# Two cross-attention layers: queries split by batch, a power on GpSimd, and layer two's residual on ScalarE and GpSimd

## The chip, the core and the metric

The kernel runs on one core of one Trainium2 chip. The metric is device time in microseconds, the median of several runs. Five engines work side by side, each in the order of its own instructions: TensorE (PE in the profile; its weight loads are PEld), VectorE (DVE), ScalarE (ACT), GpSimd (POOL) and SyncE (SP), which here only issues DMAs.

## What is computed

64 sequences x of 256 tokens and 320 channels pass through two cross-attention layers, each with a context of 77 tokens and 512 channels (the last 4 are image tokens), 20 heads of 16 channels. All is float32. Cut to what matters:

```python
# layer one (index 0 in the code): all 77 context tokens are text, its image part is empty
q, k, v = heads(x @ Wq.T), heads(text @ Wk.T), heads(text @ Wv.T)
out = softmax(q @ k.T * scale) @ v    # per head, merged
x = out @ Wo.T + bo + x
# layer two (index 1): 73 text tokens, and attention over 4 image tokens steered by it
probs_t = softmax(q @ k_t.T * scale)
text_out = probs_t @ v_t
qsem = l2norm(probs_t @ text)        # the mean context that each query saw
sem = qsem @ l2norm(ip).T
probs_ip = softmax(q @ k_ip.T * scale + 0.5 * sem) * spatial_mask
x = (text_out + probs_ip @ v_ip) @ W_out + b_out + x
```

In this data the context of both layers is the same tensor. The l2norm of `qsem` needs one over a square root for each query and head; the kernel gets the squared norm from a Gram matrix of the context.

## The kernel before

**Staging.** The 64 sequences are 32 pairs p. A pair's work is cut into units of 128 queries and eight heads; `UNITS` lists five for each of its two batches b, so ten units make a pair in each layer. The main loop (L1061) runs over steps g; p, k = divmod(g, 10), so a *period* is ten steps, k = 0 to 9, and "step 3" means k = 3. In step g layer one works on unit g and layer two on unit g - 13.

**A step, in the order in which it is written.** First `drains` (L1071): the copies and sums that take finished projections out of PSUM. Then the products of the Gram matrix for layer two (`semantics`, L769 and L776) and the scores of both layers (`scores`, L650) into one PSUM tile `sc`, which has one buffer of four banks; VectorE takes off the maxima (`shifted`, L668 and L670). Then layer two's exponentials of the step before are turned by TensorE (`transposed(1)`, L718 and L719) and copied by ScalarE (L725, L726); then ScalarE's exponential of layer one (L678), VectorE's products with the Gram part (L787, L790), the first group of `fillers`, layer one's transposes (`transposed(0)`, L718 and L719, copied at L744 and L745 or, for the fifth unit, L733 and L736), ScalarE's copy of the sums (L1057) and layer two's exponentials (L681, L682), the normalisation of layer one on VectorE and GpSimd (L695, L696, L702, L705), VectorE's sum over the products (L1130), the second group of fillers, `attend` (L807, L810, copied at L830 and L833) and the third group. In steps 9 and 4 layer two's batch 0 or 1 has its last unit, and `image_squares` (L868, L869), `text_output` (L842, three L860) and, at the step's very end, `image_norm` (L873, L875) are added; the step after has `image_scores` (L881 to L883).

**Fillers** (L950) are the projections, spread by hand over the ten steps and over three places in a step. `queries` (L584) and `project` (L597) begin with `halves` (L530): it makes eight matmuls of 128x256 (L538) for both batches at once and returns `rest` (L543), the last channels (L548), which runs in the drains of the next step. Then ScalarE copies the queries to SBUF (L593), or VectorE adds bias and residual to the output (`out_of`, L608). `project_last` (L616) makes the last 64 output channels (L623, L627). `queries` of layer two stands in step 3, that of layer one in step 4, both in the second group; `project` of layer two in step 9, with its drain in step 0; `project_last` of layer two in step 0, first group, beside the Gram matrix (`gram`, L506, copied at L509).

**What sets the order.** `keep_order` (L54) ties the instructions of PE, ACT, DVE and POOL to the order in which they are written, and those of SP up to step 13. Later DMAs of SP may be placed by the scheduler; they are issued in the order of that queue.

**PSUM.** `sc` holds four banks. Pool `ptr` has two buffers of one bank with the tag `tr`, and each `transposed` takes both: one for four transposes, one for the fifth. Pool `pms` has two buffers with the tag `ms`, for all projections and `attend` (which takes one `tr` for batch 1).

**The square root.** `image_norm` takes ScalarE's square root and behind it calls one exponential of a single element. In the trace each of the two begins with an ACT_TABLE_LOAD, at L873 and L875; the exponentials at L678 have none after it.

Of the kernel before, what the change touches and what calls it, by code (L numbers as in the profile page):

```python
# [14 lines left out]
H = 20  # L15
# [56 lines left out]
def tile_two_cross_attentions(ctx: ExitStack, tc: tile.TileContext, a: dict, out: bass.AP):  # L72
# [265 lines left out]
    def image_norms():  # L338
        sq = wkip.rearrange("p k c -> p (k c)")[:, : KE * NIP * NB].rearrange("p (k t) -> p k t", k=KE)
        nc.vector.tensor_mul(sq, cip, cip)  # L340
        ps = pms.tile([P, 512], F32, tag="ms", name="ss_ps")
        for k in range(KE):
            nc.tensor.matmul(ps[:, : NIP * NB], ones, sq[:, k, :], start=(k == 0), stop=(k == KE - 1))
        nc.vector.tensor_scalar_max(rip, ps[:, : NIP * NB], EPS * EPS)
        nc.scalar.activation(rip, rip, AF.Sqrt)
        nc.vector.reciprocal(rip, rip)


# [181 lines left out]
    def halves(name, w, src):  # L530


        main, last = src
        ps = [pms.tile([P, 2, S], F32, tag="ms", name=f"{name}_{b}") for b in range(2)]
        for b in range(2):
            for k in range(2):
                for m in range(2):
                    nc.tensor.matmul(  # L538
                        ps[b][:, m, :], w[:, k, m * P : (m + 1) * P], main[:, k, b * S : (b + 1) * S],
                        start=(k == 0 and m == 0), stop=False,  # L540
                    )

        def rest():  # L543
            for m in range(2):
                for b in range(2):
                    rows = slice(b * HALF, (b + 1) * HALF)
                    for c in halves_of(P):
                        nc.tensor.matmul(  # L548
                            ps[b][c, m, :], w[rows, 2 + b, m * P + c.start : m * P + c.stop], last[rows, :],
                            start=False, stop=(m == 1),  # L550
                        )
            return ps

        return rest

    held = {}

# [25 lines left out]

    def queries(l, p):  # L584

        rest = halves(f"q_ps{l}_{p}", wq[l], xts[p])

        def end():
            ps = rest()
            q = big.tile([P, 2, S2], F32, tag=f"q{l}", name=f"q{l}_{p}", bufs=2 - l)  # L590
            for m in range(2):
                qs[l, p, m] = q[:, m, :]
            return [lambda b=b: nc.scalar.copy(q[:, :, b * S : (b + 1) * S], ps[b]) for b in range(2)]  # L593

        held["q"] = end

    def project(l, p):  # L597

        rest = halves(f"o_ps{l}_{p}", wo[l], aTs[l, p])

        def end():
            ps = rest()

            def out_of(m):
                to = xts[p][0][:, m, :]
                for b in range(2):
                    t = to[:, b * S : (b + 1) * S]
                    nc.vector.scalar_tensor_tensor(t, ps[b][:, m, :], bo[l][:, m : m + 1], t, ALU.add, ALU.add)  # L608
                if l:
                    nc.sync.dma_start(out[m * P : (m + 1) * P, p * S2 : (p + 1) * S2], to)  # L610

            return [lambda m=m: out_of(m) for m in range(2)]

        held["o"] = end

# [177 lines left out]
    def attend(p, b):  # L793


        if (0, p) not in aTs:
            aTs[0, p] = channels("aT0", f"aT0_{p}", 1)
        main, last = aTs[0, p]
        banks = [
            pool.tile([P, 2, S], F32, tag=tag, name=f"pv{p}_{b}_{i}")  # L800
            for i, (pool, tag) in enumerate(((pms, "ms"), (ptr, "tr") if b else (pms, "ms")))
        ]

        rows = [slice(j * PAD, (j + 1) * PAD) for j in range(4)]

        def head_pairs(to, b, r, part, pt, start):
            nc.tensor.matmul(to, v0s[b][0][:, r, part].rearrange("p e d -> p (e d)"), pt, start=start, stop=False)  # L807

        def rests(to, b, r, part, rt, stop):
            nc.tensor.matmul(  # L810
                to, v0s[b][1][rows[r], part].rearrange("p e d -> p (e d)"), rt[rows[r]], start=False, stop=stop
            )

        for i in range(2):
            for j in range(4):
                r = (j + 2 * i) % 4
                head_pairs(banks[i][rows[j], 0, :], b, r, i, pts[0, i][0][:, r, :], True)
            for j in range(4 if b else 0):
                pt = pts[0, 2, j // 2][0][:, j % 2, i * P : (i + 1) * P]
                head_pairs(banks[i][rows[j], 1, :P], j // 2, j % 2, 2, pt, False)  # L820
        for j in range(4):
            for i in range(2):
                r = (j + 2 * i) % 4
                rests(banks[i][rows[j], 0, :], b, r, i, pts[0, i][1], not b)
        if b:
            for j in range(4):
                for s in range(2):
                    rests(banks[s][rows[j], 1, :P], j // 2, (j + 2 * s) % 4, 2, pts[0, 2, j // 2][1], True)
        for i in range(2):
            nc.scalar.copy(main[:, i, b * S : (b + 1) * S], banks[i][:, 0, :])  # L830
        if b:
            for s in range(2):
                nc.scalar.copy(last[:, s * P : (s + 1) * P], banks[s][:, 1, :P])  # L833
# [11 lines left out]
            lasts[p] = big.tile([P, 2, 2, H - HT, D], F32, tag="an_last", name=f"an_last{p}", bufs=1)  # L845
        by_head((an[:, 0], lasts[p][:, :, b], an[:, 1]), sums[:, :, NIP : NIP + D], rec)

    one = const.tile([P, 1], F32, tag="one", name="one")

    def by_head(to, t, factor):  # L850

# [18 lines left out]

    def image_norm(p, b):
        r = stats[p, b][2]
        nc.scalar.activation(r, r, AF.Sqrt, scale=(SCALE / SEM) ** 2)  # L873

        nc.scalar.activation(one, r[:, :1], AF.Exp, scale=0.0)  # L875

    def image_scores(p, b):

        att, sums, r = stats[p, b]
        num = nums[p, b] = small.tile(full, F32, tag="num", name=f"num{p}_{b}", bufs=2)  # L880
        nc.vector.reciprocal(r, r)  # L881
        nc.gpsimd.tensor_mul(num, sums[:, :, :NIP], r.unsqueeze(2).broadcast_to(full))
        nc.gpsimd.tensor_add(num, num, att)  # L883

# [65 lines left out]
    def fillers(k, p):  # L950
# [8 lines left out]
        if k == 0:  # L959
# [2 lines left out]
                    add(0, p, value_rows, 0, l)  # L962
                add(1, p, values, 0, p, 0)
            add(0, p - 1, gram, p - 1, 0)
            add(0, p - 3, project_last, 1, p - 3)
            if p:
                add(2, p, place_values, 0, p, 0)
            add(2, p - 1, values, 1, p - 1, 0)
# [21 lines left out]
        elif k == 3:  # L990
            add(0, p + 1, load_context, p + 1)
            if p == 0:
                add(1, p, image_keys, 0)
            add(1, p - 1, queries, 1, p - 1)
            add(1, p, place_values, 0, p, 1)
            add(1, p - 1, keys_by_head, 1, p - 1, 1)
        elif k == 4:
            if p == 0:
                add(0, p, image_keys, 1)
            add(1, p - 1, values, 1, p - 1, 1)  # L1000
            add(1, p + 1, queries, 0, p + 1)
        elif k == 5:
            if p == 0:
                add(0, p, image_keys, 2)
            add(0, p + 1, keys, 0, p + 1, 0)
            add(0, p - 1, gram, p - 1, 1)
        elif k == 6:
            while len(made_rows) * P < min(NB, 2 * (p + 2)) * T:
                rows_todo.extend((len(made_rows), l) for l in range(2))
                made_rows.append(rows_todo[-1])  # L1010
            for n in range(len(rows_todo) // 2):
                add(0, p, value_rows, *rows_todo.pop(0))
            if p == 0:
                add(0, p, image_norms)
            else:
                add(1, p, keys, 1, p, 0)
            add(0, p - 1, gram_out, 1)
            for b in range(2):
                add(1, p - 2, place_image_values, b)
        elif k == 7:  # L1020
            add(0, p + 1, keys, 0, p + 1, 1)
            add(1, p + 1, last_keys, p + 1)
            if p:
                add(2, p, keys, 1, p, 1)
            add(2, p, place_image_keys, p)
            add(1, p - 2, lambda: made.update(wT=image_transposed(p - 2)))
            if p == 0:
                add(1, p, image_rows)
        elif k == 8:
            while rows_todo:  # L1030
                add(0, p, value_rows, *rows_todo.pop(0))
            add(1, p - 1, place_gram, 1)
            add(1, p + 1, keys_by_head, 0, p + 1, 0)
            add(1, p - 1, place_values, 1, p - 1, 1)
            add(2, p - 2, lambda: held.update(i=outputs(p - 2)))
        else:
            add(0, p - 2, project, 1, p - 2)
            add(1, p + 1, values, 0, p + 1, 0)
            for b in range(2):
                add(1, p - 1, image_values, p - 1, b)  # L1040
# [9 lines left out]
    last_keys(0)  # L1050
    keys_by_head(0, 0, 0)
    queries(0, 0)
    for fn in held.pop("q")():
        fn()

# [148 lines left out]
```

## Time and profile before

| | us |
|---|---|
| median of 3 runs (2475.21 to 2477.18) | 2475.45 |
| the profiled execution | 2475.09 |
| its span in the trace | 2473.3 |
| PE busy | 2354.1 |
| DVE busy | 2001.3 |
| ACT busy | 1493.8 |
| POOL busy | 1178.5 |
| table loads of L873 and L875, 64 each of 1283 ns | 164.2 |
| L608, 256 of 461 ns | 102.7 |

The rows are read so: busy time is the sum of an engine's instructions, and an engine can be busy and still not set the end. The chain of waits follows the work that ended last back through what released it. The timeline lists instructions by start (us from the span's start), duration, engine, line, tiles written and read, and in brackets how long the engine had been idle and what ended that. The granted TensorE clock of this execution was 0.999 of full speed.

### The profile page before, as it was taken

The numbers are of one execution on the slowest core, as the hardware profiler recorded it, in microseconds if no ns is written. First come the engines' busy times: TensorE is split into PE (matmuls) and PEld (weight loads), VectorE is DVE, ScalarE is ACT, GpSimd is POOL, SyncE is SP. The second block draws the span as 40 slices with busy tenths as digits, with TensorE's granted clock in tenths as the row PEclk, the third lists the DMA queues.
The fourth block names the chain that finished last, engine by engine and source line by source line (L and its number), as shares of the span: only waits on it lengthen the run. The fifth ranks groups of instructions, "written<-read, shape, count | busy, mean of one in ns | idle before, by whom it ended". The sixth has DMA issues, their size and how long they took to land.

```text
span 2473.3 us, 97920 instructions
## 1 busy us (share of the span) xinstructions
PE 2354.1 (95%) x41374; PEld 1839.1 (74%) x41374; DVE 2001.3 (81%) x3677; ACT 1493.8 (60%) x3813; POOL 1178.5 (48%) x2621
## 2 busy tenths in 40 slices
PE   7989999999999999999999999999999999999888
PEld 5677777777777777777777777777777777777666
DVE  4588888888888888888888888888888888888864
ACT  3466666666666666666666666666666666666543
POOL 2345445545445445445545445545454545445432
PEclk9999999999999999999999999999999999999999
DMA  6202211111211111211111211111211111211000
GB/s 176 73 22 58 64 42 46 47 49 53 65 41 47 46 50 52 67 41 46 46 49 52 67 42 46 46 49 52 66 43 46 46 48 51 65 39 34 21 21 25
DMA packets 163451, 126.22 MB, mean 51 GB/s; under 512 B 72517, under 2 KB 146629, under 8 KB 163013
## 3 DMA queue, kind: packets, MB, share of 16 engines
q1 hardware_dynamic: 162148, 118.81, 16.8%
q8 instruction: 326, 5.34, 0.9%
q10 hardware_dynamic: 864, 1.15, 0.2%
q14 instruction: 113, 0.92, 0.1%
HBM read 79.56 MB, written 37.89 MB: 47 GB/s over the span
## 4 chain that ended last, share of the span: by engine, by line
PE 69%; DVE 21%; ACT 7%; issue 2%; POOL 1%; DMA 0%; SPq 0%; DVEq 0%; ACTq 0%; POOLq 0%
PE tr L718 9%; PE sc L769 8%; DVE w L670 6%; PE sc L650 6%; PE o_ps L538 5%; PE q_ps L538 5%; PE k_ps L359 4%; PE v_ps L401 4%; PE o_ps L623 4%; PE pv L807 3%; DVE mx L668 3%; PE sc L776 3%; ACT w L678 3%; PE q_ps L566 2%; DVE prod L787 2%; DVE sm L695 2%
## 5 line engine op out<-in xcount | busy, mean ns | idle before, releaser
L668 DVE TENSOR_REDUCE mx<-sc 128x8 f32<-128x584 f32 (+1 forms) x640 | 496.7, 776 | 308.7 <-PE sc L650 305.6
L670 DVE TENSOR_TENSOR w<-sc,mx 128x616 f32<-128x616 f32 x640 | 511.8, 800 | 73.4 <-ACT kT L362 0.5
L718 PE MATMUL tr<-ident,parts 128*128 128x128 f32 x2560 | 407.5, 282 | 55.7 <-ACT pt L725 49.0
L718 PEld LDWEIGHTS tr<-ident,parts 128*128 128x128 f32 x2560 | 280.2, 141 | 176.1 <-issue 76.1
L725 ACT COPY pt<-tr 128x512 f32<-128x512 f32 x320 | 187.4, 586 | 321.4 <-PE tr L718 321.4
L702 POOL TENSOR_TENSOR parts<-w,sm 128x104 f32<-128x104 f32 (+1 forms) x352 | 122.5, 352 | 536.1 <-ACT parts L682 152.6
L705 POOL TENSOR_TENSOR parts<-w,sm 128x512 f32<-128x512 f32 x320 | 337.0, 1053 | 0.0
L678 ACT ACTIVATE w<-w 128x616 f32<-128x616 f32 x320 | 229.8, 718 | 144.2 <-DVE w L670 144.2
L769 PEld LDWEIGHTS sc<-gv,pt 64*64 64x64 f32 x10240 | 232.9, 133 | 85.8 <-ACT sums L1057 31.5
L769 PE MATMUL sc<-gv,pt 64*64 64x94 f32 x10240 | 277.2, 245 | 13.2 <-ACT sums L1057 12.5
L695 DVE TENSOR_REDUCE sm<-w 128x8 f32<-128x616 f32 x320 | 251.2, 785 | 34.5 <-ACT w L678 34.5
L650 PE MATMUL sc<-kbd,q 32*64 32x154 f32 x10240 | 247.3, 293 | 1.1 <-ACT q L593 1.0
L685 POOL COPY att<-w 128x32 f32<-128x32 f32 x320 | 67.4, 210 | 377.0 <-DVE w L670 377.0
L538 PE MATMUL o_ps<-aT,wo 128*128 128x256 f32 x1024 | 231.8, 379 | 0.7 <-ACT aT L943 0.7
L538 PE MATMUL q_ps<-x,wq 128*128 128x256 f32 x1024 | 231.6, 379 | 0.0
L1130 DVE TENSOR_REDUCE nrm<-prod 128x8 f32<-128x584 f32 x320 | 226.7, 709 | 0.3
L787 DVE TENSOR_TENSOR prod<-sc,parts 128x512 f32<-128x512 f32 x320 | 217.8, 681 | 2.8 <-PE sc L776 2.8
L1057 ACT COPY sums<-sc 128x168 f32<-128x168 f32 x320 | 97.3, 304 | 200.3 <-DVE prod L790 198.5
L538 PEld LDWEIGHTS o_ps<-aT,wo 128*128 128x128 f32 x1024 | 189.6, 190 | 24.5 <-ACT aT L943 1.2
L681 ACT ACTIVATE parts<-w 128x512 f32<-128x512 f32 x320 | 207.3, 648 | 0.3 <-DVE w L670 0.2
L538 PEld LDWEIGHTS q_ps<-x,wq 128*128 128x128 f32 x1024 | 189.6, 190 | 23.1
L744 ACT COPY pt<-tr 128x512 f32<-128x512 f32 x256 | 149.6, 584 | 68.7 <-PE tr L718 68.6
(139 smaller groups left out, 4471.4 us busy)
## 6 DMA issues: line engine op xcount, KB each, us to landing
out_dram<-x SPq DMA_DIRECT2D x64, 256.0 KB
x<-in_x_dram SPq DMA_DIRECT2D x31, 512.0 KB
v_rows<-vs SPq DMA_DIRECT2D x76, 192.0 KB
vm<-v_rows SPq DMA_DIRECT2D x64, 192.0 KB
ct<-in_ctx_dram SPq DMA_DIRECT2D x32, 308.0 KB
cf<-in_ctx_dram SPq DMA_DIRECT2D x38, 256.0 KB
vq<-v_rows SPq DMA_DIRECT2D x128, 48.0 KB
v_rest<-v_rows SPq DMA_DIRECT2D x256, 9.8 KB
```

Of the source, the lines that this page charges most:

```text
L538: nc.tensor.matmul(ps[b][:, m, :], w[:, k, m * P : (m + 1) * P], main[:, k, b * S : (b + 1) * S], start=(k == 0 and m == 0), stop=False,)
L650: nc.tensor.matmul(ps[c, r, 2 * T * l : 2 * T * (l + 1)], tokens[rows, c], kbd[rows, part].rearrange("p e t -> p (e t)"), start=start, sto ...
L668: nc.vector.tensor_reduce(mx, sc[:, :, :, :nt], AX.X, ALU.max)
L670: nc.vector.tensor_tensor(w, sc, mx.unsqueeze(3).broadcast_to([P, 4, 2, T]), ALU.subtract)
L678: nc.scalar.activation(w, w, AF.Exp, scale=SCALE)
L681: nc.scalar.activation(two[:, :4].rearrange("p (e a) j t -> p (a j) e t", e=2), w[:, :, :, :M], AF.Exp, scale=SCALE)
L695: nc.vector.tensor_reduce(sm, w, AX.X, ALU.add)
L705: nc.gpsimd.tensor_tensor(two[:, : 4 * P].rearrange("p (h t) -> p h t", h=8), w[:, :, :, :M].rearrange("p j g t -> p (j g) t"), sm.rearran ...
L718: nc.tensor.transpose(ps[:, i, :], flat[:, i * P : (i + 1) * P], ident)
L769: nc.tensor.matmul(ps[c, i % 2 * 2 + j, at : at + GV], pt[half_rows, i, c], gv[b][half_rows, part, i, :], start=start and i < 2, stop=False,)
L787: nc.vector.tensor_tensor(prod[:, :, :, :M], sm[:, :, :, :M], w[:, :4].rearrange("p (e a) j t -> p (a j) e t", e=2), ALU.mult)
L1130: nc.vector.tensor_reduce(eight(stats[q, b][2], u), prod, AX.X, ALU.add)
```

## The change

1. `halves` no longer makes both batches' matmuls. It returns `batch(b)`, which takes a bank and makes the four matmuls of one batch, and `rest`. `queries` makes batch 0 where it is called; a new filler `second_batch` makes batch 1. In steps 3 and 4 `queries` moves to the first group, ahead of layer one's transposes, and `second_batch` takes its old place behind them. `project` makes both batches at once, as it did.
2. `image_norm` raises the squared norms to the power -0.5 on GpSimd (one instruction on 128x40 elements, with a constant tile `power`, issued at the end of the step, so in step 9 just ahead of step 0's drains). ScalarE's square root and its dummy exponential, and VectorE's reciprocal in `image_scores`, are gone. The constant factor moves to the one square root made at the start (L345).
3. Layer two's output is taken out of PSUM by ScalarE with the bias (two activations of 128x256 for each batch, into a tile `o` of one buffer), and GpSimd adds it to x in SBUF (128x512 for each batch). The output DMAs follow behind both. Layer one's stays on VectorE, now batch by batch.
4. `project_last` of layer two moves from the first to the second group of step 0, behind layer one's transposes. In `attend` the products of the fifth unit come behind the main products of both banks instead of between them.

```diff
@@ image_norms
-        nc.scalar.activation(rip, rip, AF.Sqrt)
+        nc.scalar.activation(rip, rip, AF.Sqrt, scale=(SCALE / SEM) ** 2)
@@ halves
-        ps = [pms.tile([P, 2, S], F32, tag="ms", name=f"{name}_{b}") for b in range(2)]
-        for b in range(2):
+        ps = []
+
+        def batch(b):
+            ps.append(pms.tile([P, 2, S], F32, tag="ms", name=f"{name}_{b}"))
             for k in range(2):
...
-        return rest
+        return batch, rest
@@ queries
-        rest = halves(f"q_ps{l}_{p}", wq[l], xts[p])
+        batch, rest = halves(f"q_ps{l}_{p}", wq[l], xts[p])
+        batch(0)
+        held["batch"] = lambda: (batch(1), held.update(q=end))
...
-        held["q"] = end
+    def second_batch():
+        held.pop("batch")()
@@ project
-            def out_of(m):
-                to = xts[p][0][:, m, :]
-                for b in range(2):
-                    t = to[:, b * S : (b + 1) * S]
+            to = xts[p][0]
+
+            def out_of(b):
+                for m in range(2):
+                    t = to[:, m, b * S : (b + 1) * S]
                     nc.vector.scalar_tensor_tensor(t, ps[b][:, m, :], bo[l][:, m : m + 1], t, ALU.add, ALU.add)
-                if l:
-                    nc.sync.dma_start(out[m * P : (m + 1) * P, p * S2 : (p + 1) * S2], to)
-
-            return [lambda m=m: out_of(m) for m in range(2)]
+
+            def with_bias(b):
+                o = big.tile([P, 2, S], F32, tag="o", name=f"o{p}_{b}", bufs=1)
+                for m in range(2):
+                    nc.scalar.activation(o[:, m], ps[b][:, m, :], AF.Identity, bias=bo[l][:, m : m + 1])
+                t = to[:, :, b * S : (b + 1) * S]
+                nc.gpsimd.tensor_tensor(t, t, o, ALU.add)
+
+            def store():
+                for m in range(2):
+                    nc.sync.dma_start(out[m * P : (m + 1) * P, p * S2 : (p + 1) * S2], to[:, m])
+
+            return [lambda b=b: (out_of, with_bias)[l](b) for b in range(2)] + [store] * l
@@ attend
-            for j in range(4 if b else 0):
+        for i in range(2 * b):
+            for j in range(4):
@@ image_norm, image_scores
-        nc.scalar.activation(r, r, AF.Sqrt, scale=(SCALE / SEM) ** 2)
-        nc.scalar.activation(one, r[:, :1], AF.Exp, scale=0.0)
+        nc.gpsimd.tensor_tensor(r, r, power, ALU.pow)
...
-        nc.vector.reciprocal(r, r)
@@ fillers
-            add(0, p - 3, project_last, 1, p - 3)
+            add(1, p - 3, project_last, 1, p - 3)
...
-            add(1, p - 1, queries, 1, p - 1)
+            add(0, p - 1, queries, 1, p - 1)
+            add(1, p - 1, second_batch)
...
-            add(1, p + 1, queries, 0, p + 1)
+            add(0, p + 1, queries, 0, p + 1)
+            add(1, p + 1, second_batch)
```

## The prediction

> **What bounds the kernel now.** I read the page's busy shares and chain first, then what TensorE waits for, then the timeline of one period around 1200 to 1282 us. A period is the ten steps of one pair of batches. The shares:
>
> ```profile
> PE 2354.1 (95%) x41374; PEld 1839.1 (74%) x41374; DVE 2001.3 (81%) x3677; ACT 1493.8 (60%) x3813; POOL 1178.5 (48%) x2621
> ...
> PE 69%; DVE 21%; ACT 7%; issue 2%; POOL 1%; DMA 0%; SPq 0%; DVEq 0%; ACTq 0%; POOLq 0%
> ```
>
> TensorE is busy 95% of the span, so all its idle time is about 119 us. What ends TensorE's waits (columns: total us, times, longest):
>
> ```profile
> PE tr L718 <- ACT pt L725: 49.0, 66, 1.9
> PE sc L769 <- ACT sums L1057: 12.5, 28, 1.6
> PE k_ps L359 <- ACT q L593: 12.5, 29, 0.4
> PE g_ps L506 <- DVE x L608: 7.0, 29, 0.6
> ```
>
> The reader is to see that the first row is the prize and that 29 is the number of full periods. In the timeline (start, us, engine, line) the first row is this, in step 3:
>
> ```profile
> 1201.99 0.59 ACT L725 COPY pt<-tr 128x512 f32<-128x512 f32 x1 [1.92 <-PE tr L718]
> ...
> 1202.72 0.63 PE L718 MATMUL tr<-ident,parts 128*128 128x128 f32 x4 [0.71 <-ACT pt L725]
> ```
>
> Layer two's transposes fill both `tr` banks, and layer one's must wait until ScalarE has emptied the first. Steps 3 and 4 each lose 0.71 us so. A period is 73.1 us (score matmuls L650 at 1208.68 and 1281.80).
>
> **Queries split by batch (steps 3 and 4).** The same 16 matmul records of L538 (3.62 us together) are issued, but half of them, about 1.7 us, now stand between the two groups of transposes. The copies end at 1202.74, and TensorE, at work until about 1203.6, no longer waits. I count 62 such places (31 and 32 query projections, the last in the drain): 62 x 0.71 = 44 us. The first bank must be free 1.7 us earlier: in step 3 its last reader ended at 1200.06 (L580), in step 4 the query copies of L593 end before the transposes do. Cover holds at both.
>
> **Power in place of square root.** ScalarE loses, twice a period, two table loads of 1.28 us (L873, L875) and two small activations (236 and 203 ns); VectorE loses a reciprocal of 353 ns. In step 9 and in most of step 4 this lies beside TensorE's work. What surfaces is in step 5: the query copies stood behind the loads until 1218.07, and the keys (L359) began at 1218.69. Moving both query halves up by 1.42 us and dropping the loads, I get keys at 1216.75 (where layer two's transposes of step 5 then end), layer one's transposes at 1218.3 (after L359 and L506), then ScalarE's two copies (0.59, 0.27), the exponential (0.72) and the sums (0.30): the next semantic matmuls (L769) start at about 1220.9 instead of 1222.63. That is 1.73, of which 1.42 is counted; 0.31 x 29 = 9 us. What is late next there is the sums copy L1057, as today. **Gains: 53 us.**
>
> The power itself stands on no row. Call it X. From below: L901, a GpSimd product of the same 128x40, 0.25 us. From above: the whole route it replaces, 1.28 + 0.24 + 1.28 + 0.20 + 0.35 = 3.35 us. I take 1.0, four passes of the nearest row, since a power is not one product. In step 5 GpSimd is idle for about 2.5 us behind it (L860 ends at 1218.36, its next work starts at 1220.88), so there X costs nothing. In step 0 it does.
>
> **Layer two's residual, and the order of step 0.** VectorE loses four L608 (1.55 us at 1251.67). ScalarE gains four activations of 128x256 and GpSimd two sums of 128x512. The tile `o` has one buffer. So the second batch's first activation waits for the first batch's sum on GpSimd, and the changed program carries that wait. GpSimd's order before that sum is text output (three L860), the power, the sum. Behind the waiting activation stand, on ScalarE, L725 and L726, which empty the banks that layer one's transposes need, then the exponential, the Gram copy and all else of step 0. Rows of the period today:
>
> ```profile
> 1251.36 0.39 DVE L842 RECIPROCAL rec<-sums 128x40 f32<-128x40 f32 x1
> ...
> 1251.89 0.63 POOL L860 TENSOR_TENSOR an<-sums,rec 128x256 f32<-128x256 f32 x1 [0.51 <-DVE rec L842]
> ...
> 1252.85 0.64 POOL L860 TENSOR_TENSOR an<-sums,rec 128x256 f32<-128x256 f32 x1
> ...
> 1253.85 0.57 ACT L725 COPY pt<-tr 128x512 f32<-128x512 f32 x1
> ...
> 1255.08 0.66 PE L718 MATMUL tr<-ident,parts 128*128 128x128 f32 x4
> ...
> 1258.22 0.88 PE L769 MATMUL sc<-gv,pt 64*64 64x94 f32 x32
> ```
>
> The reader is to see that GpSimd is occupied until 1253.49, because it waits for a reciprocal at the end of VectorE's chain; none of the edits moves that chain, which starts at step 9's scores. From there:
> - power: 1253.49 + X;
> - first sum, by L705 (128x512, 1.05 us): 1254.55 + X;
> - the second batch's two activations, by L830 (two 128x256 in 0.65 to 0.7 us): 1255.25 + X;
> - L725 (0.59): layer one's transposes start at 1255.85 + X instead of 1255.08;
> - today 3.14 us pass from there to the next L769. The last output part (L623, 1.45 us) used to stand before these transposes and now stands after them: 4.59 us. L769 at 1260.44 + X against 1258.22.
>
> Step 0 thus loses 2.2 + X, although L506 no longer waits for L608. The part 2 products moved behind in `attend` cost nothing: their copies (L733, L736) end before the main products do. The output DMAs move behind the second sum, to about 1256.6 + X; on SP's queue the Gram stores, the next values and x stand behind them, and the first consumer (x, loaded in step 2 for step 4) has over 10 us. The sums' 2.1 us on GpSimd hide before its next due work, the normalisation, which itself waits for the exponential.
>
> **The clock.** TensorE would idle from the end of L506 (about 1253.3) to 1255.85 + X, at X = 1 for 3.5 us. The trace has one stretch like this, in the drain: nothing from 2452.85 to 2455.62, 2.77 us. One-microsecond windows (PE busy first, then the other engines; PEclk is the granted clock):
>
> ```profile
> 2454.00:2455.00 1.00, 0.00 (x0) 0.00 (x0) 0.00 (x0) 0.00 (x0) 0.84 (x3) 1.00 0.00 0
> ...
> 2458.00:2459.00 1.00, 1.00 (x8) 0.67 (x7) 0.00 (x0) 0.00 (x0) 0.00 (x0) 0.50 0.00 0
> ```
>
> From about 2457.0 to 2460.5 the clock was halved, 3.5 us that give 1.75 us of work less. One sample does not say how often a stretch of 3 to 4 us does this, so none and every period are the bounds (0 and 29 x 1.75 = 51 us) and I take half, 25 us.
>
> The Trainium skill, "TensorE: Matmul & The Clock Gate", Part 1, says that the clock halves after an idle window of about 3.4 us, and that windows run freely. By that page 3.5 us of idleness would hardly ever hold a whole window, the term would be near 0, and the forecast 25 us lower; by the trace's one row, where 2.77 us sufficed, it would be 25 us higher.
>
> **The sum.** 29 x (2.2 + 1.0) = 93; clock 25; gains 53; in the tail the chain activation, sum, activation, sum (0.7 + 1.05 + 0.7 + 1.05 = 3.5) replaces four L608 (1.66): 2. Net 93 + 25 - 53 + 2 = 67. The profiled execution took 2475.09 (span 2473.3), the median of the runs is 2475.45, so they agree. **2475 + 67 = 2542 us.** Its own range: X = 0.25 and no clock term, 71 - 53 + 2 = 20, so 2495; X = 3.35 and every period halved, 161 + 51 - 53 + 2 = 161, so 2636.
>
> **Rivals.**
> - *Step 0's wait is cheaper than the splits bring (faster).* It decides at 51 / 29 = 1.76 us a period. For it: L869, just before the reciprocal, took 0.94 us at 1250.50 beside GpSimd's L705, but 0.20 elsewhere; free of that, text output starts 0.74 earlier, and with X = 0.25 step 0 loses 1.71. If the sums' wait (12.5 us, second row) also goes, the time is 2475 + 50 - 53 + 2 - 12 = 2462; with no hold-up at all 2475 - 53 - 12 = 2410. Against it: nothing here moves L705 away from L869. Chance 0.14.
> - *The two cancel*: the same without the last 12, 2475 +- 5. Chance 0.07.
> - *The power is long (slower still)*: a software routine above 3.35 us. Each us costs 29 us in step 0, and beyond 2.5 us also holds up step 5: 2640 to 2900. For it: no row bounds it truly. Against: GpSimd's rows of this shape are all 0.2 to 0.3 us. Chance 0.07.
> - *The forecast*, 2495 to 2636: 0.72.
>
> **Numbers.** The range 2470 to 2636 takes in the forecast's bounds and the cancelling case, 0.79 or so. Faster by over 0.2% (about what a measurement of this kernel can tell from no change) 0.14, within it 0.07, slower 0.79.
>
> **What would show it.** Right: no `tr` wait on L725 in steps 3 and 4; in step 0 the second batch's activation waiting for GpSimd for about 2 to 4 us, and layer one's transposes of step 0 behind L725 with a new TensorE gap of 2.5 us + X; table loads down to the first few; power's own duration read off directly; PEclk below 1 after the gap, or not. Wrong: step 0 not longer than today, which would mean that the first sum runs before 1254 or that the transposes don't stand behind it.

## The result and the profile after

| | us |
|---|---|
| before, 4 runs (2472.68 to 2477.18) | 2475.33 |
| after, 4 runs (2802.06 to 2804.03) | 2803.45 |
| ratio, 95% interval | 1.1326 [1.1306, 1.1345] |
| after, span in the trace | 2800.3 |
| after, granted TensorE clock | 0.938 of full speed |

The change costs 328 us. The direction was forecast; the size lies far above the range. The busy shares and the chain of the page after:

```profile
PE 2396.6 (86%) x41374; PEld 1865.2 (67%) x41374; DVE 1948.9 (70%) x3485; ACT 1362.1 (49%) x3685; POOL 1686.7 (60%) x2750
...
PE 54%; POOL 20%; DVE 16%; issue 5%; ACT 4%; DMA 0%; SPq 0%; POOLq 0%; DVEq 0%; ACTq 0%
```

TensorE now stands idle for 404 us (2800.3 - 2396.6) instead of 119, and GpSimd, which had 1% of the chain, has 20% of it. Line numbers have moved: `tr` is now L734 and L735 (copies L741, L742, L749), the semantic products L785, layer one's normalisation on GpSimd L718 and L721, text output L878, the sums copy L1075; new are the power (L891), the activations into `o` (L620) and the sums on GpSimd (L622). What TensorE waits for (total us, times, longest):

```profile
PE tr L734 <- ACT pt L741: 293.6, 36, 10.0
PE tr L734 <- POOL parts L721: 35.2, 27, 2.1
PE sc L785 <- ACT sums L1075: 24.8, 31, 3.6
```

Thirty of the 36 waits in the first row are one and the same place, 9.65 us in each period. The rows of the keys (12.5 us before) and of the Gram matmuls (7.0) are gone. So is the wait of steps 3 and 4, as the timeline of a step 3 shows (start, us, engine, line):

```profile
1424.67 0.59 ACT L741 COPY pt<-tr 128x512 f32<-128x512 f32 x1 [1.92 <-PE tr L734]
...
1426.25 0.60 PE L734 MATMUL tr<-ident,parts 128*128 128x128 f32 x4
```

The transposes have no bracket: TensorE came to them from the first half of the queries, which ends after the copy. The groups (busy us and mean ns, then the idle time before them) name what ScalarE waited for:

```profile
L891 POOL TENSOR_TENSOR nrm<-nrm,power 128x40 f32<-128x40 f32 x64 | 434.6, 6790 | 0.0
...
L620 ACT ACTIVATE o<-o_ps,bo 128x256 f32<-128x256 f32 x128 | 53.9, 478 | 312.0 <-POOL x L622 304.8
```

The power takes 6.79 us, 27 times the product of the same 128x40 (0.25 us). In the timeline of one step 0 the whole chain can be read downwards:

```profile
1475.02 0.63 POOL L878 TENSOR_TENSOR an<-sums,rec 128x256 f32<-128x256 f32 x1
1475.61 6.79 POOL L891 TENSOR_TENSOR nrm<-nrm,power 128x40 f32<-128x40 f32 x1
1482.37 1.25 POOL L622 TENSOR_TENSOR x<-x,o 128x512 f32<-128x512 f32 x1
1483.66 0.84 ACT L620 ACTIVATE o<-o_ps,bo 128x256 f32<-128x256 f32 x2 [9.88 <-POOL x L622]
1484.39 0.58 ACT L741 COPY pt<-tr 128x512 f32<-128x512 f32 x1
...
1485.12 1.09 PE L734 MATMUL tr<-ident,parts 128*128 128x128 f32 x4 [9.65 <-ACT pt L741]
...
1490.87 0.88 PE L785 MATMUL sc<-gv,pt 64*64 64x94 f32 x32
```

Text output ends at 1475.65; the power runs to 1482.40; only then comes the first sum, then the second batch's activations, which waited 9.88 us for the one buffer of `o`; then L741, and behind it TensorE. The clock follows (window, its length, busy time of PE, PEld, DVE, ACT, POOL, then granted clock, DMA share and GB/s):

```profile
1475.00:1477.00 2.00, 0.47 (x8) 0.32 (x5) 1.76 (x4) 0.00 (x0) 2.00 (x3) 1.00 0.00 0
1479.00:1481.00 2.00, 0.00 (x0) 0.00 (x0) 0.00 (x0) 0.00 (x0) 2.00 (x1) 0.50 0.00 0
1487.00:1488.00 1.00, 1.00 (x8) 0.54 (x6) 0.44 (x1) 0.89 (x3) 1.00 (x2) 0.50 0.44 158
1489.00:1490.00 1.00, 1.00 (x32) 0.61 (x20) 0.23 (x1) 0.00 (x0) 0.43 (x1) 1.00 0.07 14
```

TensorE's last matmul ends at 1475.48. The clock is halved from about 1478 until after 1488, so TensorE also works slowly for some 3 us once it is let go: the four transposes at 1485.12 take 1.09 us instead of the 0.66 of the prediction's row, and they do so in all 30 periods. The Trainium skill, "TensorE: Matmul & The Clock Gate", Part 1, says that the clock halves after an idle window of about 3.4 us of a free-running counter; a stretch of 9.65 us fits that in any position. But the clock was down 2.4 us after the last matmul here, and 2.1 to 4.7 us after it over the 29 full periods: idleness shorter than the page's window was enough, and the measurement decides.

Step 0 is not equally long in all periods: 18.4 us in some, 19.4 in others, 20.2 at most. The clock accounts for that. Here are two periods, in which the transposes begin at 310.87 and at 394.01, each seen some three us later:

```profile
314.00:315.00 1.00, 1.00 (x18) 0.44 (x18) 0.47 (x1) 0.00 (x0) 0.92 (x3) 1.00 0.07 11
397.00:398.00 1.00, 1.00 (x6) 0.24 (x2) 0.00 (x0) 0.00 (x0) 0.92 (x3) 0.50 0.08 16
```

In the first the clock came back 3.0 us after the transposes began, in the second 5.2; step 0 took 18.40 and 19.43 us. In all 29 full periods step 0, less half of its time at the halved clock behind the gap, is 16.8 to 17.2 us.

In step 5 the power does not hold up TensorE, but step 6 pays:

```profile
1440.10 6.80 POOL L891 TENSOR_TENSOR nrm<-nrm,power 128x40 f32<-128x40 f32 x1
...
1447.72 1.04 POOL L721 TENSOR_TENSOR parts<-w,sm 128x512 f32<-128x512 f32 x1
...
1448.82 0.66 PE L734 MATMUL tr<-ident,parts 128*128 128x128 f32 x4 [1.27 <-POOL parts L721]
...
1451.29 0.88 PE L785 MATMUL sc<-gv,pt 64*64 64x94 f32 x32 [0.70 <-ACT sums L1075]
```

Layer one's normalisation (L721) stands behind the power on GpSimd, and TensorE waits twice for what follows from it. The lengths of the steps, from a step's first score matmul to the next step's (medians over the middle of the trace, step 0 after the change the mean of 29 periods, us), put the loss in its places:

| kernel | 3 | 4 | 5 | 6 | 0 | 1 | time |
|---|---|---|---|---|---|---|---|
| before | 8.13 | 8.13 | 6.80 | 6.47 | 7.89 | 7.22 | 2475 |
| after | 7.23 | 7.23 | 6.25 | 8.33 | 18.94 | 7.23 | 2803 |

Steps 2, 7, 8 and 9 are the same in both. A period gains 2.35 us in steps 3 to 5 and loses 1.86 in step 6 and about 11.1 in step 0. In six of the 29 full periods step 6 took 8.21 us before the change already and loses next to nothing; over all 29 it loses 42 us.

### The profile page after: what moved, and what is told of

It reads as the page before. It is cut to its first block, busy times and chain, and to the rows that moved or that the text cites. A ratio compares the mean times of both kernels' runs of the same rounds, so it can differ in the third digit from the quotient of the medians.

```text
span 2800.3 us, 97864 instructions
## 1 busy us (share of the span) xinstructions
PE 2396.6 (86%) x41374; PEld 1865.2 (67%) x41374; DVE 1948.9 (70%) x3485; ACT 1362.1 (49%) x3685; POOL 1686.7 (60%) x2750
## 4 chain that ended last, share of the span: by engine, by line
PE 54%; POOL 20%; DVE 16%; issue 5%; ACT 4%; DMA 0%; SPq 0%; POOLq 0%; DVEq 0%; ACTq 0%
POOL nrm L891 12%; PE tr L734 7%; PE sc L785 6%; PE sc L666 5%; PE o_ps L639 4%; PE q_ps L540 4%; PE o_ps L540 4%; DVE w L686 4%; PE v_ps L401 3%; POOL an L878 3%; PE k_ps L359 2%; PE sc L792 2%; DVE prod L803 2%; DVE mx L684 2%; PE q_ps L568 2%
## 5 line engine op out<-in xcount | busy, mean ns | idle before, releaser
L734 PE MATMUL tr<-ident,parts 128*128 128x128 f32 x2560 | 420.4, 288 | 329.5 <-ACT pt L741 293.6
L734 PEld LDWEIGHTS tr<-ident,parts 128*128 128x128 f32 x2560 | 292.6, 144 | 442.2 <-issue 351.7
L891 POOL TENSOR_TENSOR nrm<-nrm,power 128x40 f32<-128x40 f32 x64 | 434.6, 6790 | 0.0
L718 POOL TENSOR_TENSOR parts<-w,sm 128x104 f32<-128x104 f32 (+1 forms) x352 | 121.9, 350 | 426.0 <-ACT parts L698 155.6
L741 ACT COPY pt<-tr 128x512 f32<-128x512 f32 x320 | 187.3, 585 | 357.2 <-PE tr L734 354.2
L721 POOL TENSOR_TENSOR parts<-w,sm 128x512 f32<-128x512 f32 x320 | 336.3, 1051 | 0.0
L785 PEld LDWEIGHTS sc<-gv,pt 64*64 64x64 f32 x10240 | 233.9, 133 | 103.5 <-ACT sums L1075 50.2
L785 PE MATMUL sc<-gv,pt 64*64 64x94 f32 x10240 | 278.5, 246 | 28.3 <-ACT sums L1075 24.8
L540 PE MATMUL q_ps<-x,wq 128*128 128x256 f32 x1024 | 242.1, 379 | 0.0
L620 ACT ACTIVATE o<-o_ps,bo 128x256 f32<-128x256 f32 x128 | 53.9, 478 | 312.0 <-POOL x L622 304.8
L1075 ACT COPY sums<-sc 128x168 f32<-128x168 f32 x320 | 97.5, 305 | 211.0 <-DVE prod L806 207.9
```

Of the source, the lines that this page charges most:

```text
L540: nc.tensor.matmul(ps[b][:, m, :], w[:, k, m * P : (m + 1) * P], main[:, k, b * S : (b + 1) * S], start=(k == 0 and m == 0), stop=False,)
L721: nc.gpsimd.tensor_tensor(two[:, : 4 * P].rearrange("p (h t) -> p h t", h=8), w[:, :, :, :M].rearrange("p j g t -> p (j g) t"), sm.rearran ...
L734: nc.tensor.transpose(ps[:, i, :], flat[:, i * P : (i + 1) * P], ident)
L785: nc.tensor.matmul(ps[c, i % 2 * 2 + j, at : at + GV], pt[half_rows, i, c], gv[b][half_rows, part, i, :], start=start and i < 2, stop=False,)
L891: nc.gpsimd.tensor_tensor(r, r, power, ALU.pow)
```

## The experiments

**Theory:** the forecast's mechanism is right and the power's duration is not. In step 0 the power stands ahead of the first sum, the sum ahead of the second batch's activations through the one buffer, and these ahead of TensorE; in step 6 it stands ahead of the normalisation. **Rivals:** the moved residual itself costs ScalarE and GpSimd that much (then neither another buffer nor another order helps), and the halved clock takes most of it. The table of all the kernels is at the end of this section.

### 1. Two buffers for `o`

```diff
-                o = big.tile([P, 2, S], F32, tag="o", name=f"o{p}_{b}", bufs=1)
+                o = big.tile([P, 2, S], F32, tag="o", name=f"o{p}_{b}", bufs=2)
```

> The changed kernel with two buffers for the tile o, nothing else. Theory (the power's 6.79 us reach ScalarE and TensorE through the one buffer of o): the second batch's activations no longer wait for GpSimd, layer one's transposes of step 0 stand where they stood before, and most of the 10.5 us that step 0 gained go. What stays is the power in GpSimd's own queue: the normalised tile of step 0 (L721) ends about 1 us too late for step 1, and step 6 keeps its 1.9 us. 2475 to 2540 us. Rival (GpSimd has simply too much work, 1687 us busy, and shares its memory port with VectorE): the buffer changes little, above 2700 us.

Measured: 2515.49 us, ratio 1.016 [1.0145, 1.0175], clock 0.996. One buffer more takes back 288 of the 328 us. TensorE's waits:

```profile
PE tr L734 <- POOL parts L721: 63.3, 57, 2.1
PE sc L785 <- ACT sums L1075: 46.5, 61, 3.6
```

The wait for L741 is gone (8.9 us are left), and the rows of step 6 now come 57 and 61 times instead of 27 and 31: with both sums queued behind the power, the normalisation is late in step 1 too (9.26 us instead of 7.23).

### 2. The square root back on ScalarE, `o` still of one buffer

```diff
-        nc.gpsimd.tensor_tensor(r, r, power, ALU.pow)
+        nc.scalar.activation(r, r, AF.Sqrt, scale=(SCALE / SEM) ** 2)
+        nc.scalar.activation(power[:, :1], r[:, :1], AF.Exp, scale=0.0)
...
+        nc.vector.reciprocal(r, r)
```

> The changed kernel with ScalarE's square root, its dummy exponential and VectorE's reciprocal back in place of the power; the tile o keeps its one buffer. Theory: the chain activation, sum, activation stays but is short; with the two table loads ahead of it step 0 loses about 3.9 us and the splits give back 1.8, so some 2 us a period: 2535 us, up to 2590 if the clock still halves. Rival (moving the residual to ScalarE and GpSimd is itself what costs): above 2700 us.

Measured: 2631.27 us, ratio 1.0629 [1.0611, 1.0647], clock 0.961, 41 us above the expected range. 172 us of the loss go with the power, 156 stay without it.

```profile
PE tr L734 <- ACT pt L741: 67.2, 36, 2.0
PE g_ps L506 <- ACT o L620: 59.0, 30, 2.2
PE k_ps L359 <- ACT q L597: 38.6, 29, 1.3
```

The constant factor moves back with the square root. Step 0 takes 14.1 us, 6.2 more than before, where 3.9 were expected. Behind TensorE's waits the clock is halved there for 5.4 us in the mean; half of that, 2.7 us a period or 78 in all, is an estimate of what it costs, and without it the time would lie inside the range. The second and third rows were not in the expectation: the Gram matmuls wait for a PSUM bank that the late activations empty, and the keys wait because the query copies stand behind the table loads again.

### 3. The split queries alone, on the kernel before

```diff
-        rest = halves(f"q_ps{l}_{p}", wq[l], xts[p])
+        batch, rest = halves(f"q_ps{l}_{p}", wq[l], xts[p])
+        batch(0)
+        held["batch"] = lambda: (batch(1), held.update(q=end))
...
-            add(1, p - 1, queries, 1, p - 1)
+            add(0, p - 1, queries, 1, p - 1)
+            add(1, p - 1, second_batch)
```

and the same for layer one in step 4; nothing else of the change.

> The kernel before with the split queries alone. Theory: 62 places of 0.71 us go, and step 5 keeps its table loads: 2475 - 44 = 2431 us, 2420 to 2440. Rival (half the queries between the transposes only move the wait, to the query banks or to layer one's exponentials): 2465 to 2480 us.

Measured: 2447.14 us, ratio 0.9886 [0.9871, 0.9901]; 7 us short of the range. Steps 3 and 4 fall to 7.23 us each, 0.90 less where 0.71 was forecast, but step 5 grows from 6.80 to 7.70:

```profile
PE k_ps L359 <- ACT q L597: 38.7, 29, 1.4
```

This row was 12.5 us before. TensorE comes to the keys earlier, and the query copies still stand behind the table loads on ScalarE: half of the gain turns into another wait.

### 4. The gap of step 0 filled with repeated Gram matmuls

The Gram products of step 0 are made 17 times over instead of once, so that TensorE is busy where it would idle.

```diff
+        for n in range(KE * (17 if b == 0 else 1)):
+            k = n % KE
```

> The changed kernel with the four Gram matmuls of step 0 made 17 times over (the last pass is the one that is kept), about 9 us of TensorE work inside its 9.65 us of waiting. All waits stay. Theory (the halved clock behind the gap costs 1.75 us a period): the granted clock is full again behind the gap, 2803 - 51 = 2752 us, 2740 to 2770. Rival (the clock is no part of the loss): 2803 us.

Measured: 2757.08 us, ratio 1.1137 [1.1121, 1.1154], clock 0.994. Step 0 takes 17.0 us in the mean of the 29 full periods, where it took 18.94: the halved clock was worth 1.94 us a period, 56 in all. The kernel as a whole gains only 46, because steps 0 of periods 1 and 2, which had no gap to fill, are 14 us longer with the repeated matmuls. 56 of 328 us is about a sixth: the rival that the clock takes most of the loss falls.

### 5. The power alone, on the kernel before

```diff
-        nc.scalar.activation(r, r, AF.Sqrt, scale=(SCALE / SEM) ** 2)
-        nc.scalar.activation(one, r[:, :1], AF.Exp, scale=0.0)
+        nc.gpsimd.tensor_tensor(r, r, power, ALU.pow)
...
-        nc.vector.reciprocal(r, r)
```

> The kernel before with the power on GpSimd alone (and the constant factor moved with it); queries, residual and order as before. Theory (6.79 us of power cost little in GpSimd's own queue, and much only where ScalarE waits behind it): in step 0 the normalised tile still ends before step 1 needs it; in steps 5 to 7 GpSimd is late by about 0.7 us, and the table loads' 0.43 us go: 2475 to 2500 us. Rival (the power costs its length wherever it stands): 29 periods of two powers, above 2650 us.

Measured: 2495.56 us, ratio 1.0082 [1.0067, 1.0097]. By itself the same 6.79 us cost 20 us: in the median step 5 gains 0.55, step 6 loses 0.98, step 0 stays at 7.89. Summed over the 29 full periods step 5 gives back 14 us and step 6 costs 21 (less than 29 x 0.98, since it was long in six periods before), and behind the last full period 11 more are lost.

```profile
PE tr L718 <- POOL parts L705: 15.1, 27, 2.1
```

### 6. The power behind the sums of step 0

```diff
-            image_norm(*before1[:2])
+            norms = [before1[:2]]
...
+        for ended in norms:
+            image_norm(*ended)
+        norms = []
```

The second piece stands behind the drains of the next step; `o` keeps its one buffer.

> The changed kernel with the power issued behind step 0's two sums on GpSimd instead of ahead of them; one buffer for o as before. Theory (the order power, sum, activation makes the wait): ScalarE waits for text output and one sum alone, step 0 gains about 2.6 us instead of 10.5, the power comes out late for the image scores of step 1 (1.1 us) as in step 6 (1.9 us), the splits give 2.4, the clock may still halve: 2550 to 2640 us. Rival (the place of the power does not matter): 2803 us.

Measured: 2578.47 us, ratio 1.0415 [1.0398, 1.0433], clock 0.978. Order alone gives 225 us back, with the same work on the same engines and the same buffers. Step 0 still takes 10.2 to 13.2 us: the wait through the one buffer is short now (2.9 us in most periods), but there. The spread is the clock's: in eight of the 29 full periods it stayed full and step 0 took 10.2, in the others it was halved for 2.9 to 6.3 us of work behind the wait.

```profile
PE tr L734 <- ACT pt L741: 91.2, 36, 3.2
```

### 7. Logarithm and exponential on ScalarE in place of the power, two buffers

```diff
+    nc.scalar.preload_act_table_set("natural_log_exp_and_others")
...
-        nc.gpsimd.tensor_tensor(r, r, power, ALU.pow)
+        nc.scalar.activation(r, r, AF.Ln)
+        nc.scalar.activation(r, r, AF.Exp, scale=-0.5)
```

The one square root at the start is made in the same way, and `o` has two buffers. The Trainium skill, "ScalarE: Activation LUTs", Table sets, names one set that holds both functions, so that no load is needed between them; the trace agrees, with a single load of 1.28 us.

> The changed kernel with two buffers for o, and in place of the power two ScalarE activations, a logarithm and an exponential of -0.5 times it, with the one table set that holds both preloaded at the start (the one square root of the image norms is made the same way). Theory: no table loads, no power, no wait through o: the splits give all of the 2.36 us that steps 3 to 5 lost in the changed kernel, and step 0 some 0.4: 2475 - 29 x 2.8 = 2394 us, 2385 to 2410. Rival (ScalarE and GpSimd carry too much with the residual): 2440 us or more.

Measured: 2410.15 us, ratio 0.9741 [0.9726, 0.9757]. That is at the upper edge of the range. It keeps the gains of steps 3 and 4 and pays neither loads nor power, but the 0.4 us expected from step 0 did not come. What is left in step 0 (8.08 us):

```profile
PE tr L735 <- ACT pt L742: 19.6, 35, 0.7
```

### 8. The same with layer two's residual on VectorE

```diff
-            return [lambda b=b: (out_of, with_bias)[l](b) for b in range(2)] + [store] * l
+            return [lambda b=b: out_of(b) for b in range(2)] + [store] * l
```

> The same with layer two's residual back on VectorE, batch by batch. Theory: the splits' 2.36 us a period stay, step 0 is as long as before: 2475 - 68 = 2407 us, 2400 to 2420, some 12 us behind the two-buffer kernel. Rival (VectorE's four sums do not matter, they lie beside TensorE): the same as the two-buffer kernel.

Measured: 2399.81 us, ratio 0.9694 [0.9679, 0.9708]. Expected was 12 us slower than run 7; it is 10 us faster. Step 0 takes 7.71 us instead of 8.08, and the wait for ScalarE's copy (now L742) falls from 19.6 to 3.8 us: the four bias activations stand ahead of that copy, while on VectorE the four additions delay nothing that TensorE needs. Layer two's residual on ScalarE and GpSimd is a loss of 0.37 us a period even where nobody waits for a buffer.

### 9. The power in two pieces

```diff
-        nc.gpsimd.tensor_tensor(r, r, power, ALU.pow)
+        for c in (slice(0, 10), slice(10, 2 * H)):
+            nc.gpsimd.tensor_tensor(r[:, c], r[:, c], power[:, c], ALU.pow)
```

> The changed kernel with the power issued as two instructions, of 10 and of 30 of the 40 columns. Theory: the 6.79 us are spent element by element; then the two take about 6.79 x 10 / 40 = 1.7 and 6.79 x 30 / 40 = 5.1 us, 6.8 to 7.0 together, and the time stays within 10 us of the changed kernel's 2803. Rival: most of it is spent per call (a routine that is entered, whatever the tile's size); with 3 us per call the two take 3.9 and 5.8 us, and since each us of it costs 29 us in step 0 and about as much in step 6, the time would be near 2803 + 2 x 29 x 3 = 2977.

Measured: 2830.73 us in one run, 27 above the changed kernel and outside the 10 allowed. The groups of the two pieces (busy us and mean ns):

```profile
L892 POOL TENSOR_TENSOR nrm<-nrm,power 128x30 f32<-128x30 f32 x64 | 327.1, 5110 | 0.0
L892 POOL TENSOR_TENSOR nrm<-nrm,power 128x10 f32<-128x10 f32 x64 | 126.8, 1982 | 0.0
```

20 columns more take 3.13 us more: 0.156 us a column, and about 0.42 us per call (40 columns by that 6.7, measured 6.79). Together the pieces take 7.09, 0.30 more than the one; step 6 is 0.26 us longer and step 0 0.64, of which about 0.4 is slow clock (halved for 4.9 us behind the gap in the mean instead of 4.1). The cost goes by elements, so a rival routine with a large fixed price falls.

### 10. Split queries and the new order, with the square root and the residual as before

The edit of run 2 and that of run 8 together. Beside run 3 it shows the moved `project_last` and the new order in `attend`; layer two's additions also stay batch by batch, with the output DMAs behind both.

> The changed kernel with the square root on ScalarE and layer two's residual on VectorE as they were, so that only the split queries and the new order of step zero and of attend are left; beside the split alone (2447 us) it shows that order by itself. Theory: with nothing held up on ScalarE in step 0 the order is worth a little, since the last output part stands behind the transposes: in the kernel with logarithm and exponential and the residual on VectorE step 0 took 7.71 us against 7.89 before, so 0.18 x 29 = 5 us, and the time is near 2442 (2437 to 2447). Rival: the 0.18 came from the table loads that were gone there and not from the order; then the order is worth nothing and the time is 2447 or up to 10 us above, the keys of step 5 waiting as they do with the split alone.

Measured: 2467.43 us, ratio 0.9966 [0.9952, 0.9979]. Both expectations missed: the order costs 20 us here. Step 0 takes 8.59 us instead of 7.89:

```profile
1322.72 1.28 ACT L892 ACT_TABLE_LOAD   x1
...
1324.12 0.57 ACT L741 COPY pt<-tr 128x512 f32<-128x512 f32 x1
...
1324.83 0.63 PE L734 MATMUL tr<-ident,parts 128*128 128x128 f32 x4 [1.25 <-ACT pt L741]
```

As the timelines read, the last output part used to occupy TensorE while ScalarE loaded its table and emptied the banks. Moved behind the transposes, it covers nothing.

### 11. Run 8 with the last output part ahead again

```diff
-            add(1, p - 3, project_last, 1, p - 3)
+            add(0, p - 3, project_last, 1, p - 3)
```

> The kernel with logarithm and exponential and the residual on VectorE (2400 us), with one edit: the last output part of layer two stands ahead of step 0's transposes again, as before the change. It tells whether moving it is worth anything where ScalarE has no table loads. Theory: nothing; step 0 took 7.71 us there against 7.89 before because the Gram matmuls no longer wait 0.24 us for VectorE (layer two's residual is now added batch by batch, so a bank is free sooner), and 7.89 - 0.24 = 7.65. The time is 2396 to 2403. Rival: the order itself brought the 0.18 us; then step 0 returns to 7.89 and the time is 2400 + 29 x 0.18 = 2405 or above.

Measured: 2399.03 us, ratio 0.9686 [0.9673, 0.9699], step 0 again 7.71 us. Where ScalarE has no loads, the move is worth nothing.

### 12. Power, split queries and new order, without `o`

The edit of run 8 on the changed kernel.

> The changed kernel with layer two's residual left on VectorE: split queries, power on GpSimd and the new order remain, and no tile o. Theory: in step 0 the power then holds up nobody, because nothing that ScalarE or TensorE needs soon stands behind it on GpSimd; what is left of its price is step 6, where the normalisation waits for it. Steps 5 and 6 take 6.25 and 8.35 us as in the changed kernel, against 6.46 and 6.47 in the kernel with logarithm and exponential (2400 us): 1.67 x 29 = 48, so 2448 (2440 to 2456). Rival: the power holds up step 1 as well, as it did with two buffers (9.26 us against 7.23), because it is the power and not the two sums behind it that the normalisation of step 0 waits for; then up to 2 us more a period, 2448 to 2508.

Measured: 2456.82 us, ratio 0.992 [0.9906, 0.9934], 1 us above the expected range. Steps 5 and 6 take 6.24 and 8.34 us as foreseen, step 1 7.23. Step 0 takes 7.77, 0.06 more than in run 8.

```profile
PE tr L734 <- POOL parts L721: 36.2, 27, 2.2
PE sc L785 <- ACT sums L1075: 24.3, 31, 3.6
```

These are the rows of step 6, as many times as after the change. The residual's move therefore adds 347 us to this kernel (2803 - 2457), 59 with two buffers.

All kernels with the split queries and the new order, in us:

| residual of layer two | square root | power | logarithm, exponential |
|---|---|---|---|
| VectorE | 2467 | 2457 | **2400** |
| ScalarE and GpSimd, two buffers | not tried | 2515 | 2410 |
| ScalarE and GpSimd, one buffer | 2631 | 2803 | not tried |

The last column's upper entry, run 8, beats both kernels; run 11 equals it.

## Why the prediction was wrong

**The failed step is the bound on X.** The prediction took the power at 1.0 us and gave it 3.35 at most, as the whole route that it replaces. Nothing ties the one to the other: the route's price says what the power would have to beat, not what it takes. It took 6.79. With that number in the prediction's own formula, step 0 loses 29 x (2.2 + 6.79) = 261, the clock in every period 51, less 53 of gains, and 2 in the tail: 2736, against 2803 measured. The lengths of the steps, summed over the 29 full periods, show the rest: step 0 lost 321 us (312 by the formula with the clock), steps 3 to 5 gained 66 (53), step 6 lost 42 (nothing), and behind the last full period the trace is 32 us longer (2). The rival "the power is long" had the right mechanism and the right place in step 0, named step 5 where it is step 6 that pays, and had 0.07 of the chance. The text said of it that no row bounds the power truly, and the range was drawn as if one did.

Point by point:

- **Split queries.** Right in kind, and larger in place: 0.90 us in steps 3 and 4 instead of 0.71. What the forecast left implicit is that it needs the loads gone: alone, run 3, half of it goes into the wait of the keys.
- **Step 5.** The forecast took 0.31 us beyond the 0.71 of each split. Steps 3 to 5 together gain 2.35 us a period, forecast 2 x 0.71 + 0.31 = 1.73.
- **The wait of step 0.** Right, row by row: text output, power, sum, two activations, copy, transposes. From the end of text output to L785 it gave 6.95 + X = 13.74 us; the trace has 15.22 (1475.65 to 1490.87). Of the 1.48 too little, the sum (1.25, not 1.05) and the activations (0.84, not 0.70) are 0.34; the slowed transposes (1.09, not 0.66) and output matmuls (2.35, not 1.45) are 1.33, which the forecast had in its clock term: together 1.67, a little more than is missing.
- **The clock.** Half of all periods was taken; it is every one, worth 56 us in step 0 by run 4 where 51 were the bound. The bound took 1.75 us a period from one sample; it is 1.94 in the mean, and 18.4 or 19.4 us for step 0 is a matter of when the clock came back.
- **X costs nothing in step 5 up to 2.5 us.** Longer than that it does cost, and one step later: 1.86 us in step 6 in the median.
- **The orders.** The last output part behind the transposes was in the sum, with its 1.45 us of step 0; after the change it took 2.35 us there, at the slowed clock. The same move is worth nothing in run 11, and the orders together cost 20 us in run 10. The order in `attend` was priced at nothing; no run shows it by itself.
- **VectorE's relief.** Its residual lay beside other work, as the prediction had it; run 8 beside run 7 shows that the move does not pay even with two buffers and without the power.

Of the 32 us behind the last full period, 11.5 are one more step 0 with the same wait (19.4 us instead of 7.9), 8 the last step 0 (13.2 instead of 5.2), and 6 the wait of TensorE for the last weights of the image attention, ahead of which the last power stands: 8.8 us (L928) instead of 2.8 (L913). The other 7 stay open.

## What to carry to other kernels

An operation that no row of the trace shows has no upper bound from the work that it replaces; measure it by itself, or let the range hold the case that it is many times longer, with every place where something stands behind it priced. Before a long instruction is put on an engine that is mostly idle, list what is queued behind it there: the same 6.79 us cost 20 us by themselves (run 5), while behind them the residual through one buffer made the kernel 347 us slower (run 12 beside the change); an order or a second buffer took back 225 and 288 of that. Where two functions of ScalarE alternate, look for one table set that holds both before moving either to another engine.

## What the runs showed of the hardware

- GpSimd's power on 128x40 elements takes 6.79 us, 0.156 us a column plus about 0.42 a call; its product of the same shape 0.25.
- The logarithm and the exponential run from one preloaded table set: one load of 1.28 us in the whole execution instead of two a step that ends a batch.
- GpSimd's sum of 128x512 (L622) takes 1.26 us where its product of that shape (L721) takes 1.05; the tiles read differ too.
- After the change the clock was halved 2.1 to 4.7 us after TensorE's last matmul in step 0 and came back 2.9 to 6.1 us after its work began again. In run 6 a stretch of 2.9 to 3.2 us was enough for that in 21 of 29 periods.
